# Pairwise bilinear products: from batch rows on the partitions to products computed transposed, with W stationary

## The chip, the core and the metric

The kernel runs on one NeuronCore of a Trainium2 chip. The core has five engines with queues of their own: TensorE (PE; its weight loads are PEld), VectorE (DVE), ScalarE (ACT), GpSimd (POOL) and SyncE (SP). Transfers between the device's memory (DRAM) and the on-chip memory (SBUF, 128 partitions) are issued from the queues of SP, ACT and POOL and carried by 16 DMA engines. TensorE writes its results to PSUM, which has eight banks of 512 float32 per partition. The metric is the device time of one execution in microseconds; work on the host isn't in it.

## The reference

The input is x, 4096 batch rows of 32 fields with 64 numbers each, and W, one 64 x 64 matrix for each of the 496 pairs of fields i < j. For each batch row and each pair, the vector of field i is multiplied with the pair's matrix, and the result elementwise with the vector of field j:

```python
i_idx, j_idx = np.triu_indices(32, k=1)
vi = inputs[:, i_idx, :]                      # (4096, 496, 64)
vj = inputs[:, j_idx, :]
vdotw = jnp.einsum('bpd,pde->bpe', vi, W)     # W: (496, 64, 64)
return (vdotw * vj).reshape(4096, -1)         # (4096, 31744)
```

All is float32. The output has 4096 x 31744 numbers, 520 MB; x has 33.6 MB and W 8.1 MB.

## The kernel before, in words

Batch rows lie on the partitions. The batch is cut into 32 tiles `t` of 128 rows. The output is kept as it is needed: for each row, the pairs in order, so that for a field i the columns of all j > i stand side by side.

**x.** `load_x` brings x in by 17 loads (`x_slots`, L35): one tile, fifteen times two tiles, and one. They land in `xbuf`, which has room for three tiles. A load of two tiles has 128 rows of 16,384 bytes. Most are issued on ACT's queue (L169). The six in `LIGHT_LOADS` go by POOL's queue through `load_beside` (L144) instead: two transfers that are cut so that the DMA engine numbered `LIGHT` carries none of it, since its eight rows are given in fours to two other engines. `PAIRS_FROM` says which two, in turn. Ahead of each of the two transfers, `from_engine` issues a small one ("nudge", L127) that moves POOL's round of engines to the one wanted. POOL's transfers are kept in program order.

**Transposes.** TensorE contracts over the partitions, so the 64 numbers of a field must lie on the partitions. `transpose_x` (L185) turns half a tile at a time: eight transposes of 128 x 128 on TensorE (L190) into two PSUM banks, and one copy by ScalarE to `xT` (L191). `xT` holds two fields per 128 columns, an even field on partitions 0 to 63 and the next on 64 to 127. The second half of a tile is turned at field pair `p` = 3, the first half of the next tile at `p` = 9 (L250 to L253).

**Products.** For a field pair `p` (fields 2p and 2p+1), the loop at L255 goes over the columns of W in pieces of up to 512. The stationary operand is 64 x 128 of `xT`, the moving one 64 x n of W, in SBUF as a whole (`w_sb`); the product lands as 128 batch rows x n columns (L262). The two fields use the two halves of TensorE's rows and two banks of the PSUM ring `pring`, so up to four steps are in flight. `multiply` (L195) lets DVE multiply both banks at once with the columns of x that stand beside (L203). Where the pieces of the two fields don't match, or where the ring wraps, it is done in parts (L203 again, or L211), which is why there are many shapes.

**Stores.** DVE writes into `ring`, 440 x 64 columns of SBUF. As soon as a third of it (147 or 146 units of 64 columns; in the first round four smaller parts) is written, `made` (L218) issues one store of 128 rows on SP's queue (L225). DVE may write into a third again when its store has landed.

**Start.** The first x tile and the next two go out on ACT's queue, W in five steps (six transfers) on SP's (L238, L240); the stores come behind W on SP's queue. A framework places the waits between engines from the order in which the program is written; each engine works in the order of the program.

On the host, x and W are only rearranged (L291 to L310).

Of the kernel before, what the change touches and what calls it, by code (L numbers as in the profile page):

```python
# [12 lines left out]
P = 128  # L13
# [3 lines left out]
ROUND = [147, 147, 146]  # L17
FIRST_ROUND = [118, 102, 110, 110]

LOADS = [[0], [1], [2, 3], [4, 5, 6], [7, 8, 9, 10, 11, 12, 13, 14, 15]]  # L20


FIRST_HALF_AT, SECOND_HALF_AT = 9, 3
RING_UNITS = sum(ROUND)
# [3 lines left out]
LIGHT_LOADS = [3, 5, 8, 10, 13, 15]  # L28
PAIRS_FROM = [5, 7, 9, 11, 13, 15, 1, 2, 0, 14, 12, 10, 8, 6]
HEAD = P // DMA_ENGINES  # L30
REST = HEAD // 2
PAD = 16


def x_slots(NT):  # L35


    loads = [[(0, 0)]]
    for t in range(1, NT, 2):
        if t + 1 == NT:  # L40
            loads.append([(t, 1)])
        elif loads[-1][-1] == (t - 1, 2):
            loads.append([(t + 1, 0), (t, 1)])
        else:
            loads.append([(t, 1), (t + 1, 2)])
    return loads
# [3 lines left out]
def pair_bilinear_kernel(  # L50
# [4 lines left out]
    out: bass.AP,  # L55
    F: int,
# [3 lines left out]

    nc = tc.nc
    NT = out.shape[1] * 2 // (F * (F - 1) * D)
    NPR = F // 2

    width = [(F - 1 - i) * D for i in range(F)]
    off = [sum(width[:i]) for i in range(F)]
    cols = sum(width)


    woff = [i % 2 * D + sum(width[i % 2 : i : 2]) for i in range(F)]
    ring_w = RING_UNITS * D
    ends = [0]
    while ends[-1] < NT * cols:
        for units in ROUND if ends[-1] else FIRST_ROUND:
            ends.append(min(ends[-1] + units * D, NT * cols))
            if ends[-1] == NT * cols:
                break
    missing = [b - a for a, b in zip(ends, ends[1:])]  # L100
    stored = 0
# [3 lines left out]

    ident = const.tile([P, P], F32, tag="ident", name="ident")
    make_identity(nc, ident)

    def runs(tl, a, b, n):

        ap = tl[:, a : a + n]
        return bass.AP(ap.tensor, ap.offset, [list(ap.ap[0]), [b - a, 2], list(ap.ap[1])])

    xbuf = const.tile([P, 3 * F * D], F32, tag="x", name="x")
    x_loads = x_slots(NT)
    pads = (DMA_ENGINES + 1) * PAD
    x_sizes = [
        P * len(load) * F * D + (pads if i in LIGHT_LOADS else 0) for i, load in enumerate(x_loads)
    ]
    slot = {t: xbuf[:, ts(s, F * D)] for load in x_loads for t, s in load}  # L120
# [8 lines left out]
    def from_engine(e):  # L129

        nonlocal cursor
        k = (e - cursor) % DMA_ENGINES
        if k:
            nudge = nudges[e == LIGHT + 1]
            if k == 1:
                from_pool(nudge[:3, :8], x[:64].rearrange("(g c) -> g c", g=2)[:, :12])
            else:
                from_pool(
                    nudge[:k].rearrange("p (h c) -> p h c", h=2)[:, :, :4],
                    x[: k * 8].rearrange("(p h c) -> p h c", p=k, h=2),  # L140
                )
        cursor = e

    def load_beside(at, xt, n_row, lap):  # L144

        nonlocal cursor
        most = DMA_ENGINES - 1
        for e, k, rows, p in (
            (PAIRS_FROM[lap % len(PAIRS_FROM)], 2, REST, most * HEAD),
            (LIGHT + 1, most, HEAD, 0),  # L150
        ):
            from_engine(e)
            n = rows * n_row
            blocks = x[at : at + k * (n + PAD)].rearrange("(k c) -> k c", k=k)
            from_pool(xt[p : p + k * rows], blocks[:, :n])
            at += k * (n + PAD)
            cursor = (e + k) % DMA_ENGINES

    def load_x(load):

        i = x_loads.index(load)
        at = sum(x_sizes[:i])
        n = len(load) * F * D
        s = load[0][1]
        xt = xbuf[:, s * F * D : s * F * D + n]
        if i in LIGHT_LOADS:
            load_beside(at, xt, n, LIGHT_LOADS.index(i))
        else:
            nc.scalar.dma_start(out=xt, in_=x[at : at + P * n].rearrange("(p c) -> p c", p=P))  # L169

# [3 lines left out]
    def take_banks(n):  # L174

        nonlocal bank
        if bank + n > BANKS:
            bank = 0
# [4 lines left out]
    xT = const.tile([P, NPR * P], F32, tag="xT", name="xT")  # L183

    def transpose_x(xt, g):  # L185

        n = 2 * BANK // P
        pt = take_banks(2)
        for c in range(n):
            nc.tensor.transpose(pt[:, ts(c, P)], xt[:, ts(n * g + c, P)], ident)  # L190
        nc.scalar.copy(xT[:, ts(g, 2 * BANK)], pt)  # L191

    ring = const.tile([P, ring_w], F32, tag="ring", name="ring")

    def multiply(tos, pm, xj, n):  # L195

        at = [to % ring_w for to in tos]
        cuts = {ring_w - a for a in at if a < ring_w < a + n}
        for i, j in zip([0, *sorted(cuts)], [*sorted(cuts), n]):
            a = [(to + i) % ring_w for to in tos]  # L200
            if len(tos) == 2 and a[0] < a[1]:
                xs = xj[:, i:j]
                nc.vector.tensor_tensor(  # L203
                    runs(ring, a[0], a[1], j - i),
                    runs(pm, i, BANK + i, j - i),
                    bass.AP(xs.tensor, xs.offset, [xs.ap[0], [0, 2], xs.ap[1]]),
                    ALU.mult,
                )
                continue
            for h, b in enumerate(a):  # L210
                nc.vector.tensor_tensor(  # L211
                    ring[:, b : b + j - i],
                    pm[:, h * BANK + i : h * BANK + j],
                    xj[:, i:j],
                    ALU.mult,
                )

    def made(a, b):  # L218

        nonlocal stored  # L220
        for i in range(stored, len(missing)):
            missing[i] -= max(0, min(b, ends[i + 1]) - max(a, ends[i]))
        while stored < len(missing) and not missing[stored]:
            a, b = ends[stored : stored + 2]
            nc.sync.dma_start(  # L225
                out=out[:, a:b], in_=ring[:, a % ring_w : a % ring_w + b - a]
            )
            stored += 1

    load_x(x_loads[0])  # L230
    w_sb = const.tile([P, sum(width[0::2])], F32, tag="w", name="w")
    done = 0
    for g in LOADS:

        upto = woff[2 * g[-1]] + width[2 * g[-1]]
        odd = woff[F - 1] + width[F - 1]
        both = min(upto, odd)
        nc.sync.dma_start(out=w_sb[:, done:both], in_=w[:, done:both])  # L238
        if both < upto:
            nc.sync.dma_start(out=w_sb[:D, both:upto], in_=w[:D, both:upto])  # L240
        done = upto

    transpose_x(slot[0], 0)
    for t in range(NT):
        xt = slot[t]
        for load in x_loads:
            if min(load)[0] == t + 1:
                load_x(load)
# [71 lines left out]
```

## Time and profile before

| | |
|---|---|
| time, median of 6 runs (lowest to highest) | 1319.6 us (1316.84 to 1319.89) |
| the profiled execution's own time | 1319.79 us |
| its span, first to last instruction | 1318.0 us |
| TensorE's granted clock | 0.962 |
| busy: PE, DVE, ACT, POOL | 1173.4, 1188.6, 66.1, 14.4 us |
| moved by DMA | 562.64 MB, 427 GB/s over the span |
| HBM read, written | 41.70 MB, 520.09 MB |
| matmul records on TensorE: products (L262), transposes (L190) | 4864, 512 |
| DVE instructions: L203, L211 | 1012, 471 |
| stores issued (L225) | 110 |

How to read it: the page gives each engine's busy time and its share of the span, then cuts the span into 40 equal slices (33 us here) with a digit for the busy tenths of each. "DMA" is the mean busy share of the 16 DMA engines, "GB/s" what they moved. The DMA queues are listed with packets, MB and their share of the time of 16 engines: q1 is SP's, q10 ACT's, q0 POOL's, q8 and q14 fetch instructions and tables. A chain is followed back from the last instruction, and its shares of the span are given by engine. A group of instructions is one line of the kernel, engine, operation and shape: number of instructions | busy time, mean ns of one | idle time of the engine before them, and what ended most of it. A float32 product shows as two records, each with a weight load. The mean of one is its latency, which is longer than the distance at which instructions follow each other. In a table of windows each row is a stretch of the span: its length, then the busy time of PE, PEld, DVE, ACT and POOL with the number of instructions, the granted clock, the DMA share and GB/s. A wait is given as engine, line <- what it waited for: total us, times, longest.

### The profile page before, as it was taken

The page shows a single profiled execution, that of the slowest core. Times are in us where ns is not written, and L with a number is a line of the kernel's source. Part 1 is how long each engine was busy: PE and PEld are TensorE (multiplying, and loading weights), DVE is VectorE, ACT ScalarE, POOL GpSimd, SP SyncE. Part 2 cuts the span into 40 slices and gives each one's busy share as a digit, 9 for nine tenths or more (in the row PEclk, how much of TensorE's full clock was granted, in tenths as well). Part 3 has the DMA queues.
Part 4 walks back from the last instruction along what each step waited for, and adds up shares of the span by engine and source line. Part 5 has one row for each costly group of instructions (what it writes and reads, how often), then busy time and mean ns, then how long its engine had stood idle before and what let it go on. Part 6 is the DMA issues. An engine that isn't in the chain of part 4 may idle for free.

```text
span 1318.0 us, 13125 instructions
## 1 busy us (share of the span) xinstructions
PE 1173.4 (89%) x5376; PEld 562.2 (43%) x5376; DVE 1188.6 (90%) x1483; ACT 66.1 (5%) x65; POOL 14.4 (1%) x30
## 2 busy tenths in 40 slices
PE   7999988989899998988989989898997989989992
PEld 3444335443444443444444444444444444434441
DVE  5999988989899998988989989898997999979993
ACT  1000000000000000000000000000000000000000
POOL 0000000000000000000000000000000000000000
PEclk9999998989899999998999989899998999989997
DMA  9999999999999999999999999999999999999998
GB/s 394 432 431 434 428 415 432 430 434 435 417 430 430 431 433 432 431 427 434 427 431 434 422 434 426 430 434 426 430 431 420 430 415 431 431 429 429 429 431 373
DMA packets 20012, 562.64 MB, mean 427 GB/s; under 512 B 2992, under 2 KB 2992, under 8 KB 3312
## 3 DMA queue, kind: packets, MB, share of 16 engines
q1 hardware_dynamic: 16640, 528.24, 93.4%
q10 hardware_dynamic: 1584, 20.97, 3.8%
q0 software_dynamic: 1728, 12.59, 2.4%
q8 instruction: 42, 0.69, 0.2%
q14 instruction: 18, 0.15, 0.0%
HBM read 41.70 MB, written 520.09 MB: 426 GB/s over the span
## 4 chain that ended last, share of the span: by engine, by line
DMA 44%; DVE 40%; issue 8%; PE 6%; POOL 0%; DVEq 0%; ACT 0%
DMA out_dram<-ring 36%; DVE ring L203 33%; DMA x<-in_x_dram 8%; DVE ring L211 7%; PE pring L262 5%; PE pring L190 1%; DVEq L203 0%; POOL x L127 0%; POOL nudge L127 0%; ACT xT L191 0%; DVEq L316 0%; DVEq L211 0%
## 5 line engine op out<-in xcount | busy, mean ns | idle before, releaser
L262 PE MATMUL pring<-w,xT 64*128 64x512 f32 (+4 forms) x4864 | 1108.9, 563 | 95.4 <-DVE ring L203 68.8
L203 DVE TENSOR_TENSOR ring<-pring,x 128x1024 f32<-128x1024 f32 (+4 forms) x1012 | 1043.5, 1092 | 79.5 <-DMA out_dram<-ring 44.4
L262 PEld LDWEIGHTS pring<-w,xT 64*128 64x128 f32 x4864 | 505.3, 191 | 656.8 <-DVE ring L203 441.7
L211 DVE TENSOR_TENSOR ring<-pring,x 128x64 f32<-128x64 f32 (+7 forms) x471 | 168.6, 412 | 28.6 <-DMA out_dram<-ring 20.4
L191 ACT COPY xT<-pring 128x1024 f32<-128x1024 f32 x64 | 64.8, 1012 | 1203.6 <-PE pring L190 1164.5
L190 PE MATMUL pring<-ident,x 128*128 128x128 f32 x512 | 72.6, 286 | 25.8 <-DMA x<-in_x_dram 17.3
L190 PEld LDWEIGHTS pring<-ident,x 128*128 128x128 f32 x512 | 56.9, 144 | 75.5 <-DVE ring L203 53.1
L127 POOL DMA_DIRECT2D x<-in_x_dram x12 | 7.0, 586 | 1125.2 <-DVE ring L211 1125.2
L127 POOL DMA_DIRECT2D nudge<-in_x_dram x12 | 6.8, 566 | 0.3 <-issue 0.3
L191 ACT ACT_TABLE_LOAD x1 | 1.3, 1283 | 1.7 <-PEq L312 1.7
masks.py:199 POOL TENSOR_SCALAR_AFFINE_SELECT ident<-ident 128x128 f32<-128x128 f32 x1 | 0.3, 287 | 0.1
masks.py:197 POOL MEMSET ident<- 128x128 f32 x1 | 0.2, 204 | 0.3 <-POOLq L312 0.3
L312 POOL MEMSET const-bfloat16-1.0<- 128x1 bf16 x1 | 0.1, 101 | 0.0
L312 POOL MEMSET const-uint8-127<- 128x1 uint8 x1 | 0.1, 101 | 0.0
L312 POOL MEMSET const-float32-0.0<- 128x1 f32 x1 | 0.1, 98 | 0.2 <-issue 0.2
L312 POOL MEMSET const-float32-1.0<- 128x1 f32 x1 | 0.1, 98 | 0.0
## 6 DMA issues: line engine op xcount, KB each, us to landing
out_dram<-ring SPq DMA_DIRECT2D x70, 4704.0 KB, 20.6
out_dram<-ring SPq DMA_DIRECT2D x35, 4672.0 KB, 21.0
x<-in_x_dram ACTq DMA_DIRECT2D x9, 2048.0 KB, 20.9
x<-in_x_dram POOLq DMA_DIRECT2D x6, 1920.0 KB, 31.5
out_dram<-ring SPq DMA_DIRECT2D x2, 3520.0 KB, 17.1
out_dram<-ring SPq DMA_DIRECT2D x1, 3776.0 KB, 17.3
out_dram<-ring SPq DMA_DIRECT2D x1, 3264.0 KB, 17.6
w<-in_w_dram SPq DMA_DIRECT2D x1, 2112.0 KB, 26.9
```

Source lines behind the costliest of these rows:

```text
L127: tc.keep_in_program_order(nc.gpsimd.dma_start(out=out, in_=in_))
L190: nc.tensor.transpose(pt[:, ts(c, P)], xt[:, ts(n * g + c, P)], ident)
L191: nc.scalar.copy(xT[:, ts(g, 2 * BANK)], pt)
L203: nc.vector.tensor_tensor(runs(ring, a[0], a[1], j - i), runs(pm, i, BANK + i, j - i), bass.AP(xs.tensor, xs.offset, [xs.ap[0], [0, 2], xs ...
L211: nc.vector.tensor_tensor(ring[:, b : b + j - i], pm[:, h * BANK + i : h * BANK + j], xj[:, i:j], ALU.mult,)
L262: nc.tensor.matmul(pm[:, h * BANK : h * BANK + n], xT[h * D : (h + 1) * D, ts(p, P)], w_sb[h * D : (h + 1) * D, a : a + n], start=True, st ...
L312: nc = bacc.Bacc("TRN2", target_bir_lowering=False, num_devices=1)
```

## The change

The products are computed transposed: the columns of one W matrix lie on the partitions of the result, and the batch rows along its columns.

- The host hands over x transposed: `xbuf` holds, for one chunk of 512 batch rows, 16 pieces (field pairs) of 512 columns, each with two fields on the two halves of the partitions. Which field is on which half alternates with the pair (`row_half`). There are eight chunks (`NC`) in place of 32 tiles. The same copy of x is TensorE's moving operand and DVE's multiplier; the transposes, the identity, ScalarE's copies and `xT` are gone.
- W is the stationary operand: for a step of two field pairs p < q, two products of 64 x 128 with 64 x 512 (field 2p and 2p+1, each with both fields of q), on the two halves of TensorE's rows. A step within pairs, (p, None), does two pairs of 64 x 64 in each of its two banks, and needs two DVE instructions on half the partitions each, where the other steps need one. `steps_of` gives 124 steps per chunk, in groups of four field pairs: the group with itself, then with each later group.
- x is loaded by 32 loads of 1 MB (a chunk's group of four pairs; 128 rows of 8,192 bytes). The four of chunk 0 go out first, on ACT's queue. A group of the next chunk is loaded over the old one when the last step that reads it has been issued. Nine loads go by POOL's queue as before (`LIGHT_LOADS`).
- The ring is three tiles of 20, 18 and 18 blocks of 512 columns, each stored as a whole by one transfer on SP's queue (in two halves in the first round). A tile is written again when its store has landed.
- W is loaded in five steps of 8, 16, 24, 32 and 44 blocks of 128 columns. The output leaves the chip in the order of the steps; the host puts it in order.

The diff, cut to its core:

```diff
-ROUND = [147, 147, 146]
-FIRST_ROUND = [118, 102, 110, 110]
-LOADS = [[0], [1], [2, 3], [4, 5, 6], [7, 8, 9, 10, 11, 12, 13, 14, 15]]
-FIRST_HALF_AT, SECOND_HALF_AT = 9, 3
-RING_UNITS = sum(ROUND)
+GROUP = 4
+W_STEPS = [8, 16, 24, 32, 44]
+SLOTS = [20, 18, 18]
 DMA_ENGINES = 16
 LIGHT = 4
-LIGHT_LOADS = [3, 5, 8, 10, 13, 15]
-PAIRS_FROM = [5, 7, 9, 11, 13, 15, 1, 2, 0, 14, 12, 10, 8, 6]
+LIGHT_LOADS = [(1, 0), (2, 0), (3, 0), (3, 2), (4, 0), (5, 0), (6, 0), (6, 2), (7, 0)]
+PAIRS_FROM = [5, 7, 9, 11, 13, 15, 1, 6, 8]
...
+def steps_of(NPR):
+    steps = []
+    for g in range(0, NPR, GROUP):
+        steps.append((g, None))
+        for h in range(g, NPR, GROUP):
+            for p in range(g, g + GROUP):
+                steps += [(p, q) for q in range(max(h, p + 1), h + GROUP)]
+    return steps
+
+def row_half(p, i):
+    return (i + p) % 2
+
+def x_loads(B, NPR):
+    return [(c, g) for c in range(B // BANK) for g in range(NPR // GROUP)]
...
+    xbuf = const.tile([P, NPR * BANK], F32, tag="x", name="x")
+    for g in range(NPR // GROUP):
+        load_x((0, g))
+    w_sb = const.tile([P, len(steps) * P], F32, tag="w", name="w")
+    done = 0
+    for n in W_STEPS:
+        cols = slice(done * P, (done + n) * P)
+        nc.sync.dma_start(out=w_sb[:, cols], in_=w[:, cols])
+        done += n
...
-        for c in range(n):
-            nc.tensor.transpose(pt[:, ts(c, P)], xt[:, ts(n * g + c, P)], ident)
-        nc.scalar.copy(xT[:, ts(g, 2 * BANK)], pt)
...
+    for c in range(NC):
+        for s, (p, q) in enumerate(steps):
+            pm = take_banks(2)
+            if made == base + room:
+                turn += 1
+                base, room = made, SLOTS[turn % len(SLOTS)]
+                tag = f"slot{turn % len(SLOTS)}"
+                osb = ring.tile([P, room * BANK], F32, tag=tag, name=tag)
+            a = (made - base) * BANK
+            for k in range(2):
+                if q is None:
+                    for h in range(2):
+                        pair = p + 2 * k + h
+                        m = row_half(pair, 2 * pair)
+                        o = row_half(pair, 2 * pair + 1)
+                        nc.tensor.matmul(
+                            pm[o * D : (o + 1) * D, ts(k, BANK)],
+                            w_sb[m * D : (m + 1) * D, s * P + k * D : s * P + (k + 1) * D],
+                            x_of(pair, m), start=True, stop=True)
+                else:
+                    m = row_half(p, 2 * p + k)
+                    nc.tensor.matmul(pm[:, ts(k, BANK)], w_sb[m * D : (m + 1) * D, ts(s, P)],
+                                     x_of(p, m), start=True, stop=True)
+            if q is None:
+                for h in range(2):
+                    rows = slice(h * D, (h + 1) * D)
+                    nc.vector.tensor_tensor(
+                        strided(osb[rows, a : a + BANK], BANK), strided(pm[rows, :BANK], BANK),
+                        strided(x_of(p + 1 - h, h), 2 * BANK), ALU.mult)
+            else:
+                nc.vector.tensor_tensor(
+                    strided(osb[:, a : a + BANK], BANK), strided(pm[:, :BANK], BANK),
+                    strided(x_of(q), 0), ALU.mult)
+            made += 2
+            half = turn < len(SLOTS) and made - base == (room // 2 + 1) // 2 * 2
+            if half or made in (base + room, blocks):
+                nc.sync.dma_start(out=out[:, stored * BANK : made * BANK],
+                                  in_=osb[:, (stored - base) * BANK : (made - base) * BANK])
+                stored = made
+            last = s + 1 == len(steps) or steps[s + 1][0] // GROUP != p // GROUP
+            if last and c + 1 < NC:
+                load_x((c + 1, p // GROUP))
```

`x_of(p, h)` is the piece of pair p in `xbuf` (all partitions, or half h), `strided(ap, step)` the same columns twice at a distance of `step`. `load_beside`, `from_engine` and `load_x` work as before, on the new loads.

## The prediction

> **What bounds the kernel now.** I read the page's slices first, then the DMA queues, then the chain that ended last.
>
> ```profile
> DMA  9999999999999999999999999999999999999998
> GB/s 394 432 431 434 428 415 432 430 434 435 417 430 430 431 433 432 431 427 434 427 431 434 422 434 426 430 434 426 430 431 420 430 415 431 431 429 429 429 431 373
> DMA packets 20012, 562.64 MB, mean 427 GB/s; under 512 B 2992, under 2 KB 2992, under 8 KB 3312
> q1 hardware_dynamic: 16640, 528.24, 93.4%
> q10 hardware_dynamic: 1584, 20.97, 3.8%
> q0 software_dynamic: 1728, 12.59, 2.4%
> q8 instruction: 42, 0.69, 0.2%
> DMA 44%; DVE 40%; issue 8%; PE 6%; POOL 0%; DVEq 0%; ACT 0%
> ```
>
> The row of nines says that the DMA engines are full from the first slice to the last but one, at 430 GB/s give or take a few. The output alone is 520 MB. The chain names VectorE (DVE) for 40%, so next: has DVE room?
>
> ```profile
> L203 DVE TENSOR_TENSOR ring<-pring,x 128x1024 f32<-128x1024 f32 x708 | 833.8, 1217 | 40.1 <-DMA out_dram<-ring 21.2 <-PE pring L262 8.2 <-DVE ring L203 1.2
> L262 PE MATMUL pring<-w,xT 64*128 64x512 f32 x3072 | 858.6, 635 | 75.0 <-DVE ring L203 57.1 <-DVE ring L211 12.3
> ...
> 1272.01 12.47 DVE L203 TENSOR_TENSOR ring<-pring,x 128x1024 f32<-128x1024 f32 x12
> ...
> DVE ring L203 <- DMA out_dram<-ring: 44.4, 19, 7.2
> ...
> PE pring L190 <- DMA x<-in_x_dram: 17.3, 4, 8.5
> ```
>
> The first two are groups by form, the third the timeline of DVE, the last the list of waits. Running freely, DVE makes a 128x1024 product in 12.47/12 = 1.04 us; it is busy 1188.6 us of 1318 and waits 44.4 + 20.4 us for stores (L203, L211). So DVE is ahead of the stores, but not by much. The windows show where the DMA engines lose (last columns: DMA share, GB/s):
>
> ```profile
> 40.00:88.00 48.00, 45.51 (x225) 21.72 (x222) 47.55 (x63) 3.04 (x3) 0.00 (x0) 1.00 1.01 434
> 173.00:200.00 27.00, 21.00 (x94) 8.05 (x92) 20.00 (x23) 1.01 (x1) 0.00 (x0) 0.94 1.02 415
> 254.00:270.00 16.00, 14.40 (x67) 6.60 (x66) 13.71 (x17) 1.01 (x1) 0.00 (x0) 1.00 1.00 432
> 337.00:363.00 26.00, 21.44 (x88) 10.22 (x88) 21.45 (x23) 1.01 (x1) 0.00 (x0) 0.87 1.01 421
> 1012.00:1032.00 20.00, 19.49 (x90) 10.72 (x91) 17.76 (x27) 0.98 (x1) 0.00 (x0) 0.90 0.97 417
> 1063.00:1081.00 18.00, 16.89 (x80) 6.86 (x78) 17.75 (x19) 1.01 (x1) 0.00 (x0) 1.00 1.01 421
> 1224.00:1238.00 14.00, 13.37 (x62) 5.73 (x58) 13.11 (x18) 1.01 (x1) 0.00 (x0) 1.00 1.00 422
> 1297.00:1318.00 21.00, 0.00 (x0) 0.00 (x0) 0.00 (x0) 0.00 (x0) 0.00 (x0) 0.56 0.79 339
> ```
>
> Stores alone run at 432 to 434 (1240:1297 has 432); I take 433. While x comes in through POOL's queue (173, 337) the rate falls to 415 and 421 with the share still at 1.0: packets take longer. Through ACT's queue the loss is small (254: none) to middling (1063, 1224). At 1012:1032 the share is 0.97: some engines have no store. The waits of that stretch say why: POOL's x landed after 32.9 us, the transposes (L190) waited 4.4 us for it, and DVE 5.4 us for TensorE.
>
> An account of the span: 562.64 MB / 433 GB/s = 1299.4 us. Head, 393 GB/s over the first 32 us: 40/433 x 32 = 3.0. Last 21 us, 339 GB/s: 4.6. The six POOL loads (windows from 173, 337, 577, 737, 980, 1143; 415, 421, 424, 422, 422, 426 GB/s over 25 to 28 us): 4.2. The nine ACT loads in mid-run (432, 432, 431, 433, 423, 420, 424, 421, 422 GB/s over 14 to 21 us): 2.2. The late stretch at 1012: 0.7. Sum 1314.1; 3.9 of 1318.0 stays unassigned, in small dips. The execution took 1319.79 us, 1.8 more than its span; the median of the six is 1319.6, so I add 1.6 to a span.
>
> **What the Trainium skill says.** "DMA: Bandwidth & Descriptors", section "Where 436 GB/s comes from", gives 435.2 GB/s as the ceiling of the 16 ports: the trace's 430 to 435 agrees, so the rate has no room. Its "Issuing engines are not separate DMA queues" says that SP's, ACT's and POOL's transfers share the same 16 engines; the trace agrees (share 1.0 with one queue or two). "Queues, rings and completion order" says that an engine alternates between queues packet by packet; I use this for how long a load lasts beside stores, and the trace's landings (20.9 us for 2048 KB by ACT) fit it.
>
> **The change part by part.**
>
> Bytes. Output and x are the same. W is 124 x 128 x 128 x 4 B = 8.13 MB; the six W loads add up to 7952 KB = 8.14 MB. The instruction queues bring 0.84 MB; q8's 0.69 MB is 10752 x 64 B, TensorE's 5376 + 5376 records. A product is two records before (2432 products, 4864 records). After there are 8 x (120 x 2 + 4 x 4) = 2048 products, so 8192 records: 0.16 MB less, with DVE's and ACT's some 0.2 MB, 0.46 us. Before, the lightened POOL loads spare one engine 6 x 8 x 16,384 B = 0.79 MB; after, 9 x 8 x 8,192 B = 0.59 MB: also 0.2 MB less. If that engine does the fetching, the gain is nil; I count -0.2 (0 to -0.46).
>
> x rows of 8,192 instead of 16,384 B. In the trace's packet records 16,384 B take 611 ns and 8,192 B 309: 7 ns more for two halves. Rows go from 2176 to 4096: 1920 x 7 / 16 engines = +0.8 us.
>
> x loads beside stores. In mid-run POOL goes from six of 2.1 MB to nine of 1.05, ACT from nine (eight of 2.1 MB, one of 1.05) to nineteen of 1.05. If the loss goes with bytes: POOL 4.2 x 0.75 = 3.2, ACT 2.2 x 19.9/17.8 = 2.5, together -0.7. If with the number of loads: POOL 4.2 x 9/6 = 6.3, ACT 2.2 x 19/9 = 4.6, together +4.5. For bytes: POOL loads lose over their whole 25 us and ACT's mostly nothing, so it is something each packet meets. For number: the only 1 MB load in mid-run, at 1224, lost 11/433 x 14 = 0.36 us, as much as a load of 2 MB. I take bytes, and keep +4.5 as the other end.
>
> DVE and TensorE. DVE: 8 x (120 + 4 x 2) = 1024 products of 1024 columns (the diagonal ones on half the partitions, at full price) x 1.04 = 1065 us against 1188.6 now; at the busy mean of 833.8/708 = 1.18 it would be 1206. TensorE: 3072 records of 64x512 were busy 858.6 us, so 1.12 for a pair of products (four records) with back-pressure; 992 pairs plus 32 more for the diagonals make 1145. Transposes (72.6) and ScalarE's copies (64.8) go. All stay below 1299, covered by the stores; without that cover DVE's gain would be up to 124. What it and the earlier x (below) buy is the late stretch: -0.7.
>
> Ring. 56 blocks of 2 KB per partition against 55 before, in 3 slots; a slot is free only when its store has landed. DVE needs 28 x 1.03 x 1.04 = 30 us for a round, the stores 56 x 0.262 MB / 433 = 34 plus loads. Two slots (some 23 us) lie queued. Nothing lost.
>
> Head. The first multiply no longer waits for transposes and copy (first transpose 8.48, first DVE 13.43 us). But stores stand behind W on SP's queue, and x and W are now 4.19 + 8.13 = 12.3 MB = 28.5 us of DMA from some 2 us on, against 11.3 MB. The first ten blocks need six DVE instructions, done by about 17 us: the store waits for the queue, not the reverse. Same bytes overall: 0 (-0.5 to +0.5). The four ACT and five SP issues are some 0.5 us each, hidden by the transfers.
>
> Reloads. A load waits on ACT's or POOL's queue for DVE's last use; nothing else is queued there but later loads. At 1318/992 = 1.33 us per step the shortest notice is group 8's: seven steps to the chunk's end and 23 of the next, 40 us (group 4: 37 steps, 49 us). Estimate of a landing: 8 rows per engine, each behind a store row of 40,960 B (1392 ns x 40,960/37,632 = 1.52): 8 x 1.83 = 15 us, 22 where two engines take 12 rows; POOL's loads of twice the bytes took 31.5 us (median) to 32.9. In time, so no stretch like 1012.
>
> Tail. The last store is 4 blocks, 8,192 B rows, as now: 0. Stores are 110 in both.
>
> Sum: -0.2 + 0.8 - 0.7 - 0.7 = -0.8: span 1317.2, time 1318.8.
>
> **Rivals.** (1) Faster: the loss beside loads comes from engines out of step after late stores, and goes as DVE gains room. For it: the dip at 1063 follows the late stretch at 1012. Against it: the load at 337 loses 0.7 us although DVE is ahead there and waits 3.8 us for a store. Two thirds of 6.4, and 1.0 of the unassigned: -0.2 + 0.8 - 0.7 - 4.3 - 1.0 = -5.4, 1314.2. (2) Slower: each load has a fixed price, so 28 in mid-run cost more than 15: -0.2 + 0.8 - 0.7 + 4.5 = +4.4, 1324.0. It decides (+2.6 us) from an extra 2.7 us, 0.21 for each of 13 further loads; 0.36 was seen for one. (3) A reload comes late and TensorE stops; the queued slots hide 20 us, beyond that each of 7 chunks pays. At 5 us each: 1354. The 40 us of notice speak against it. (4) One DMA engine ends late because the lightening no longer matches the fetches: 0.2 MB on one engine is 0.2/27 GB/s = 7 us; if half of it shows, 1323. The equal 0.2 MB above speak against it. That the change would leave the transposes or the extra copies in isn't possible by its code.
>
> **How the numbers follow.** No change can be told from about 0.2% (2.6 us; the six runs lie within 3.1). Mine: 0.50, with its own range 1316 to 1321.5; rival 1: 0.25; rival 2: 0.15; rival 3: 0.03; rival 4: 0.07. Mine is mostly "same" (0.42) with 0.06 faster and 0.02 slower. Rival 1 is faster (0.24), rivals 2 and 4 slower or just within (0.03). Faster 0.30, same 0.46, slower 0.24. The range, 1313.5 to 1324.5, holds nearly all of mine, two thirds of rival 1 and half of 2 and 4.
>
> **What would show it.** The row of nines unchanged; DVE busy near 1065 with long waits for stores (over 150 us); no window with a DMA share below 0.99 between head and tail; POOL-load windows of about 415 to 425 GB/s but shorter; no TensorE wait for x after the head. Wrong: a mid-run rate of stores alone other than 433, reload waits on TensorE, a last stretch in which few engines still move bytes, or 28 dips as deep as the old 15.

## The result, and the profile after

The changed kernel takes 1315.28 us (median of 16 runs, 1314.29 to 1316.73) against 1318.65 us for the kernel before (36 runs, 1316.47 to 1323.29; the six of the table above are among them): the ratio is 0.9975, 95% interval 0.9969 to 0.9982. That is 3.4 us less. The forecast was 1318.8 us with a range of 1313.5 to 1324.5; its likeliest case had 0.8 us of gain. The profiled execution took 1315.93 us with a span of 1313.8 us.

The page of the changed kernel, its slices, queues and chain:

```profile
DMA  9999999999999999999999999999999999999998
GB/s 392 430 437 429 433 430 434 431 432 430 436 428 434 430 428 428 431 431 428 435 425 440 423 436 426 437 430 427 435 424 434 428 431 431 424 434 434 432 433 354
DMA packets 22507, 562.41 MB, mean 428 GB/s; under 512 B 3648, under 2 KB 3648, under 8 KB 3776
q1 hardware_dynamic: 16560, 528.23, 93.6%
q10 hardware_dynamic: 3312, 24.12, 4.4%
q0 software_dynamic: 2592, 9.45, 1.8%
q8 instruction: 32, 0.52, 0.1%
DMA 65%; DVE 31%; issue 1%; PE 1%; DVEq 0%
```

The row of nines is unchanged: the DMA engines still bound the kernel. What differs is small. The lowest mid-run slice is 423 GB/s, where it was 415. The instruction fetches on q8 are 32 packets, where they were 42. The last slice is lower, 354 GB/s after 373. In the chain, DMA's share went from 44% to 65%, DVE's from 40% to 31%.

Groups by line, DVE's timeline near the end, and the list of waits:

```profile
L207 DVE TENSOR_TENSOR slot<-pring,x 128x1024 f32<-128x1024 f32 x960 | 1095.6, 1216 | 105.4 <-DMA out_dram<-slot 98.6
L200 DVE TENSOR_TENSOR slot<-pring,x 64x1024 f32<-64x1024 f32 x64 | 77.9, 1218 | 14.8 <-PE pring L181 11.5
...
1242.54 11.41 DVE L207 TENSOR_TENSOR slot<-pring,x 128x1024 f32<-128x1024 f32 x10 [1.79 <-DMA out_dram<-slot]
...
DVE slot L207 <- DMA out_dram<-slot: 98.6, 62, 5.2
PE pring L181 <- DMA x<-in_x_dram: 7.6, 1, 7.6
```

DVE makes ten products in 11.41 us, 1.14 us each, and is busy 1171.2 us in all, 17 us less than before and not 124 less. The diagonal products on 64 partitions (L200) cost the same 1.22 us of latency as those on 128. DVE waits 98.6 us for stores (L207) where it waited 44.4 + 20.4. TensorE waits for x once, in the head.

The windows of the changed kernel (length, busy PE, PEld, DVE, POOL, clock, DMA share, GB/s):

```profile
0.00:32.00 32.00, 24.41 (x84) 7.14 (x84) 20.66 (x19) 0.88 (x5) 1.00 0.96 391
159.00:186.00 27.00, 24.72 (x96) 7.45 (x96) 25.93 (x23) 0.00 (x0) 0.99 1.00 427
241.00:264.00 23.00, 19.19 (x68) 5.12 (x68) 19.86 (x19) 0.00 (x0) 1.00 1.01 432
319.00:347.00 28.00, 22.69 (x86) 7.25 (x84) 25.06 (x23) 0.00 (x0) 0.94 1.02 437
481.00:510.00 29.00, 23.64 (x84) 6.88 (x84) 25.11 (x23) 0.00 (x0) 0.90 1.00 420
967.00:994.00 27.00, 21.08 (x80) 5.76 (x76) 21.69 (x20) 0.00 (x0) 0.97 1.01 422
1046.00:1071.00 25.00, 21.55 (x78) 6.72 (x76) 22.82 (x21) 0.00 (x0) 0.93 0.99 423
1240.00:1290.00 50.00, 43.40 (x160) 12.74 (x156) 47.44 (x42) 0.00 (x0) 0.97 1.00 433
1297.00:1313.80 16.80, 0.00 (x0) 0.00 (x0) 0.00 (x0) 0.00 (x0) 0.50 0.64 275
```

A POOL load that runs alone costs nothing in one place (241, 432 GB/s) and some in another (1046, 423), and ACT's loads (159, 319) cost nothing to a little. The two deep dips left, 420 and 422, are where a POOL load and an ACT load run at the same time (loads (3, 2) with (3, 3), and (6, 2) with (6, 3)). The last 16.8 us move only 275 GB/s; the last 16.8 us of the kernel before moved 316.

An account that needs no reference rate comes from the packet records of the traces. Packets of 8,192 B and 37,632 B have a usual duration of 309 and 1392 ns, which gives 7.6 ns + 36.8 ps per byte; what a packet takes beyond this is its lengthening. A row of a transfer is one packet here. All is us, a mean over the 16 engines; fetches overlap with stores on their engine, and what is counted twice is taken off. The sum is the time of the last store packet.

| us | before | after | e6 | e8 | e2 | e7 | e11 |
|---|---|---|---|---|---|---|---|
| packets at their usual duration | 1301.4 | 1302.6 | 1301.4 | 1302.9 | 1301.3 | 1302.4 | 1301.3 |
| instruction and table fetches | 2.9 | 2.1 | 2.6 | 2.8 | 2.1 | 2.1 | 2.1 |
| lengthening in the first 32 us | 1.4 | 1.3 | 1.3 | 1.4 | 1.1 | 1.2 | 1.0 |
| lengthening of x rows after it | 2.5 | 0.2 | 1.8 | 1.8 | 0.9 | 0.1 | 0.9 |
| of store rows beside loads | 4.8 | 3.4 | 4.4 | 4.5 | 3.7 | 2.4 | 3.9 |
| of store rows elsewhere | 2.7 | 1.9 | 2.5 | 2.0 | 2.0 | 1.8 | 2.1 |
| counted twice | -4.4 | -5.0 | -4.4 | -4.9 | -4.6 | -4.9 | -4.6 |
| engines idle in the first 30 us | 2.0 | 2.0 | 2.1 | 2.0 | 2.2 | 2.2 | 2.2 |
| idle in between | 1.0 | 0.0 | 0.2 | 0.3 | 0.1 | 0.0 | 0.2 |
| idle in the last 25 us | 2.6 | 3.6 | 2.9 | 3.1 | 5.1 | 2.7 | 6.0 |
| end of the last store packet | 1316.7 | 1312.2 | 1314.7 | 1315.9 | 1314.1 | 1310.1 | 1315.2 |

(e2 to e11 are experiments below.) From before to after: x rows -2.3, stores beside loads -1.4, stores elsewhere -0.8, idle in between -1.0, fetches -0.8; against it more rows and semaphores +1.2 and a longer end +1.0 (the rest is mostly what is counted twice).

Each column is one execution, and executions differ: the profiled one of the kernel before took 1319.79 us, 1.1 more than the median, that of e11 1.9 more than its own, that of e8 1.7 less. Experiments that leave a kernel nearly as it was show how much one column can tell. By the same reckoning e9 (the kernel before with other store rows) has x rows lengthened by 2.0 us, store rows by 6.1 where the kernel before has 4.8 + 2.7, 0.3 us idle in between, 2.7 at the end, and its last store packet ends at 1314.2. Near copies of the changed kernel (e3, e5b, e10) have 0.2 to 0.3, 4.5 to 5.5, 0.0 and 4.1 to 4.2, and end at 1312.0 to 1313.1. So what repeats is that x rows are held up less, that fetches take less, and that the end is longer. More than a microsecond of the difference in store rows, and most of the idle time in between, is no larger than what the kernel before and its near copy differ by.

### The profile page after: what moved, and what is told of

It is laid out like the page before. It is cut to its first block, busy times and chain, and to the rows that moved or that the text cites. A ratio compares the mean times of both kernels' runs of the same rounds, so it can differ in the third digit from the quotient of the medians.

```text
span 1313.8 us, 9765 instructions
## 1 busy us (share of the span) xinstructions
PE 1137.7 (87%) x4096; PEld 335.0 (25%) x4096; DVE 1171.2 (89%) x1024; POOL 20.7 (2%) x40
## 2 busy tenths in 40 slices
DMA packets 22507, 562.41 MB, mean 428 GB/s; under 512 B 3648, under 2 KB 3648, under 8 KB 3776
## 4 chain that ended last, share of the span: by engine, by line
DMA 65%; DVE 31%; issue 1%; PE 1%; DVEq 0%
DMA out_dram<-slot 64%; DVE slot L207 29%; DVE slot L200 2%; DMA x<-in_x_dram 1%; PE pring L181 1%; PE pring L190 0%; DVEq L207 0%; DVEq L269 0%; DVEq L200 0%
## 5 line engine op out<-in xcount | busy, mean ns | idle before, releaser
L190 PE MATMUL pring<-x,w 64*128 64x512 f32 x3840 | 1074.3, 655 | 140.9 <-DVE slot L207 105.4
L207 DVE TENSOR_TENSOR slot<-pring,x 128x1024 f32<-128x1024 f32 x960 | 1095.6, 1216 | 105.4 <-DMA out_dram<-slot 98.6
L190 PEld LDWEIGHTS pring<-x,w 64*128 64x128 f32 x3840 | 319.1, 193 | 896.7 <-DVE slot L207 764.9
L200 DVE TENSOR_TENSOR slot<-pring,x 64x1024 f32<-64x1024 f32 x64 | 77.9, 1218 | 14.8 <-PE pring L181 11.5
L181 PE MATMUL pring<-x,w 64*64 64x512 f32 x256 | 66.1, 638 | 9.3 <-DMA x<-in_x_dram 7.6
L181 PEld LDWEIGHTS pring<-x,w 64*64 64x64 f32 x256 | 15.9, 139 | 55.5 <-DVE slot L207 26.8
L91 POOL DMA_DIRECT2D x<-in_x_dram x18 | 10.5, 585 | 1021.6 <-PE pring L190 1021.6
L91 POOL DMA_DIRECT2D nudge<-in_x_dram x18 | 10.1, 562 | 0.9 <-POOLq L265 0.9
## 6 DMA issues: line engine op xcount, KB each, us to landing
x<-in_x_dram ACTq DMA_DIRECT2D x23, 1024.0 KB, 18.6
x<-in_x_dram POOLq DMA_DIRECT2D x9, 960.0 KB, 28.2
```

The costliest lines, as they stand in the source:

```text
L91: tc.keep_in_program_order(nc.gpsimd.dma_start(out=out, in_=in_))
L181: nc.tensor.matmul(pm[o * D : (o + 1) * D, ts(k, BANK)], w_sb[m * D : (m + 1) * D, s * P + k * D : s * P + (k + 1) * D], x_of(pair, m), st ...
L190: nc.tensor.matmul(pm[:, ts(k, BANK)], w_sb[m * D : (m + 1) * D, ts(s, P)], x_of(p, m), start=True, stop=True,)
L200: nc.vector.tensor_tensor(strided(osb[rows, a : a + BANK], BANK), strided(pm[rows, :BANK], BANK), strided(x_of(p + 1 - h, h), 2 * BANK), A ...
L207: nc.vector.tensor_tensor(strided(osb[:, a : a + BANK], BANK), strided(pm[:, :BANK], BANK), strided(x_of(q), 0), ALU.mult,)
```

## The experiments

Three theories were set against each other (a fourth, C, between A and B, is stated with e8). A: the loads of x became smaller (1 MB, rows of 8,192 B), and that alone is the gain. B: the gain is what transposed products take away (transposes, late x, DVE's time). D, formed later: the gain is that store rows now begin at round addresses. Unless a kernel is named, "changed" means the changed kernel.

**Small loads in the kernel before.**

```diff
-    loads = [[(0, 0)]]
-    for t in range(1, NT, 2):
...
+    loads = [[(t, t % 3)] for t in range(NT)]
-LIGHT_LOADS = [3, 5, 8, 10, 13, 15]
-PAIRS_FROM = [5, 7, 9, 11, 13, 15, 1, 2, 0, 14, 12, 10, 8, 6]
+LIGHT_LOADS = [2, 5, 7, 10, 12, 15, 17, 20, 22, 25, 27, 30]
+PAIRS_FROM = [5, 7, 9, 11, 13, 15, 1, 6, 8, 10, 12, 14]
```

> The kernel before, but x in 32 loads of one tile (1 MB, rows of 8,192 B; twelve of them by POOL's queue) in place of 15 of two tiles; nothing else. Theory A: the loss beside loads comes from the size of the loads, and the changed kernel's gain is their halving; then this takes 1315 to 1316.5 us, the windows beside loads rise to 428 to 433 GB/s, the account's 6.4 us beside loads falls to under 4. Theory B: the gain comes from what the transposed products take away (transposes, late x, DVE's many shapes); then this stays at 1318 to 1319.5 us with dips as before.

It took 1322.06 us, ratio 1.0031 (1.0020 to 1.0041), outside what any theory expected. The windows of this kernel's head show why:

```profile
0.00:14.00 14.00, 3.28 (x12) 2.41 (x14) 0.00 (x0) 2.29 (x2) 3.64 (x11) 1.00 0.92 320
14.00:24.00 10.00, 8.29 (x30) 3.20 (x26) 8.26 (x8) 0.00 (x0) 0.00 (x0) 1.00 0.97 242
```

Tile 2's place in `xbuf` is free from the start, so its load, POOL's, went out at once and ran beside W: 242 GB/s with the engines busy, and the first slice fell from 394 to 326 GB/s. In the account, the lengthening in the first 32 us is 6.3 us in place of 1.4. So this run can't decide on A. It was repeated with the first POOL load later (e8):

```diff
-LIGHT_LOADS = [2, 5, 7, 10, 12, 15, 17, 20, 22, 25, 27, 30]
+LIGHT_LOADS = [4, 7, 9, 12, 14, 17, 19, 22, 24, 26, 28, 30]
```

> As the kernel before with 32 loads of one tile, but the first POOL load is that of tile 4, so that none runs beside W in the head (there the first slice had fallen from 394 to 326 GB/s, 5 us). The rest of that run lost less beside its loads than the kernel before. Theory C (load size is worth 1 to 2 us, less 0.8 for the extra rows; the rest of the gain is from the transposed products): 1316.5 to 1318 us. Theory A (it is the whole gain): 1315 to 1316 us. Theory B (load size is worth nothing): 1319 to 1320 us, for the extra rows.

1320.67 us, ratio 1.0013 (1.0002 to 1.0024): a little above even what B expected; small loads by themselves don't make the kernel before faster. A falls, and C (1316.5 to 1318) with it. Its 14 runs scatter widely, from 1317.56 to 1326.28 us, for a reason not looked for, and the profiled one is among the faster. In the table above the rows of x in this run are lengthened by 1.8 us, and 0.8 of it falls in one load, at 905 us, in a stretch in which stores run a little short (the engines' idle time in between is 0.3 us for the whole run):

```profile
0.00:32.00 32.00, 21.71 (x94) 10.50 (x96) 17.47 (x18) 3.31 (x3) 1.39 (x7) 1.00 0.96 392
870.00:930.00 60.00, 57.20 (x254) 28.39 (x253) 57.27 (x73) 3.77 (x4) 2.26 (x4) 0.95 1.00 420
```

**Big loads in the changed kernel.** (The change is in six places; its core:)

```diff
-    return [(c, g) for c in range(B // BANK) for g in range(NPR // GROUP)]
+    return [(c, g) for c in range(B // BANK) for g in range(0, NPR // GROUP, 2 if c else 1)]
-LIGHT_LOADS = [(1, 0), (2, 0), (3, 0), (3, 2), (4, 0), (5, 0), (6, 0), (6, 2), (7, 0)]
+LIGHT_LOADS = [(1, 0), (2, 0), (4, 0), (5, 0), (7, 0)]
...
-                load_x((c + 1, p // GROUP))
+                if p // GROUP % 2:
+                    load_x((c + 1, p // GROUP - 1))
```

> The changed kernel, but from the second chunk on x in loads of two groups (2 MB, rows of 16,384 B, five of them by POOL's queue); nothing else. Theory A: the loss comes back, 1317.5 to 1319 us, windows beside POOL loads at 415 to 426 GB/s. Theory B: 1315 to 1316 us as the changed kernel. A reload that comes too late would show as TensorE waiting for x in the later chunks.

1316.51 us, ratio 0.9982 (0.9973 to 0.9991), between the two; the interval overlaps the changed kernel's. The dips beside POOL loads are back, in the size that A expected:

```profile
127.00:155.00 28.00, 20.93 (x76) 5.42 (x72) 21.58 (x20) 0.00 (x0) 0.93 1.00 420
610.00:638.00 28.00, 23.40 (x84) 7.25 (x84) 22.59 (x20) 0.00 (x0) 0.94 1.00 420
```

but 1.3 us less for rows and semaphores make up for part of them, and most of the gain over the kernel before stays. TensorE waited for x in the head only. The edit also changes the balance of the engines: its five POOL loads keep 0.66 MB off the spared engine, where the changed kernel's nine keep 0.59 MB off it, and the engines are idle 5.1 us at the end in place of 3.6. What of its microsecond belongs to the size and what to the balance can't be told from it.

**Two POOL loads moved.**

```diff
-LIGHT_LOADS = [(1, 0), (2, 0), (3, 0), (3, 2), (4, 0), (5, 0), (6, 0), (6, 2), (7, 0)]
+LIGHT_LOADS = [(1, 0), (2, 0), (3, 0), (3, 1), (4, 0), (5, 0), (6, 0), (6, 1), (7, 0)]
```

> The changed kernel, but the two POOL loads (3, 2) and (6, 2), which run beside ACT's load of the next group, are (3, 1) and (6, 1), which run alone. Theory A (loss grows with the share of reads at one time): the dips of 420 and 422 GB/s at 481 and 967 us go, 1313.5 to 1314.5 us. Theory B: no difference, 1315.3 us.

1314.98 us, ratio 0.9977 (0.9967 to 0.9987): no difference from the changed kernel that this can tell. The dips themselves went, as this kernel's windows show:

```profile
481.00:510.00 29.00, 25.68 (x88) 7.67 (x88) 27.24 (x24) 0.00 (x0) 0.88 1.02 434
967.00:994.00 27.00, 21.62 (x82) 6.03 (x80) 22.70 (x20) 0.00 (x0) 0.96 1.01 432
```

In the account, store rows beside loads were lengthened by 2.8 us in place of 3.4, and the engines were idle 4.1 us at the end in place of 3.6. A reading that fits, but was not tested: what a dip gives back to some engines doesn't shorten the run if another engine is the last.

**The kernel before without transposes.** Those of later tiles are left out, so that W is multiplied with tile 0's rows for every tile; the output is another.

```diff
-            if p == SECOND_HALF_AT:
+            if p == SECOND_HALF_AT and not t:
-            if p == FIRST_HALF_AT and t + 1 < NT:
+            if p == FIRST_HALF_AT and t + 1 < 1:
```

> The kernel before with the transposes and copies of the first half tile alone and the second half of tile 0; the others are left out, so that later tiles are multiplied with tile 0's transposed rows, and the output is another. x is still loaded and multiplied with. Theory A: only the late stretch goes, 1317.5 to 1319 us. Theory B: most of the gain, 1315 to 1316 us.

1317.93 us, ratio 0.9998 (0.9989 to 1.0006), where B expected 1315 to 1316. The transposes and copies were worth at most 1.5 us, though TensorE did 41 us less. Windows of this kernel:

```profile
173.00:200.00 27.00, 20.61 (x88) 7.33 (x86) 21.18 (x25) 0.00 (x0) 0.00 (x0) 0.95 1.00 422
1012.00:1032.00 20.00, 19.28 (x86) 9.50 (x86) 19.36 (x25) 0.00 (x0) 0.00 (x0) 0.89 0.99 427
1063.00:1081.00 18.00, 13.87 (x58) 5.48 (x54) 14.21 (x16) 0.00 (x0) 0.00 (x0) 0.91 1.02 440
```

The stretch at 1012 no longer has late stores (427 GB/s for 417, and 440 for 421 at 1063). The dip beside the POOL load at 173 (422) stays. That the late stretch came with the transposes, as the prediction read it, isn't shown by this: e9 below keeps them, and its profile has no such stretch either.

**A burden on DVE.** Twice; the first was placed badly.

```diff
+            if s % 4 == 0:
+                nc.vector.tensor_tensor(spare, spare, spare, ALU.mult)
             made += 2
```

> The changed kernel with one more DVE product of 128x64 on a spare tile every fourth step (248 of them, some 0.13 us each, 32 us in all), left out of the output. DVE's busy time goes from 1171 to about 1203 us, above the 1188.6 us of the kernel before. If DVE's room is what the change gained by, 1318 to 1320 us; if not, 1315 to 1316 us.

1347.01 us, ratio 1.0211 (1.0198 to 1.0224). The added products depend on nothing but each other, and the framework put them early. DVE's timeline of this kernel, and two windows:

```profile
60.26 0.74 DVE L216 TENSOR_TENSOR spare<-spare 128x64 f32<-128x64 f32 x3
60.92 1.22 DVE L209 TENSOR_TENSOR slot<-pring,x 128x1024 f32<-128x1024 f32 x1
62.05 0.47 DVE L216 TENSOR_TENSOR spare<-spare 128x64 f32<-128x64 f32 x2
...
60.00:90.00 30.00, 19.98 (x72) 5.43 (x72) 28.97 (x67) 0.00 (x0) 1.00 0.60 259
300.00:400.00 100.00, 88.78 (x326) 26.39 (x325) 92.25 (x82) 0.00 (x0) 0.97 1.00 430
```

Two or three of them stand behind every product from 60 to 160 us. All 248 start before 153 us. DVE then needs some 1.7 us for two blocks where the stores need 1.2, so it falls behind the stores, and the DMA share falls to 0.60. Elsewhere nothing is lost (430 GB/s). It shows what DVE costs where it does bound, and not what its room is worth. So it was tied to the step:

```diff
+            if s % 8 == 1:
+                nc.vector.tensor_tensor(spare, pm[:, :64], x_of(p)[:, :64], ALU.mult)
             made += 2
```

> The changed kernel with a further DVE product of 128x64 after every eighth step (128 of them, some 0.2 us each, 26 us), on the step's own bank and a spare tile, so that it stays in its place; left out of the output. DVE's busy time then is 1195 to 1200 us, a little over the 1188.6 of the kernel before. If DVE's 17 us less are what the change gained by: 1318 to 1320 us. If not: 1315 to 1316 us, with DVE's waits for stores down from 101 to about 75 us.

1316.37 us, ratio 0.9981 (0.9974 to 0.9989). The page's first part and a wait:

```profile
PE 1139.8 (87%) x4096; PEld 328.6 (25%) x4096; DVE 1186.9 (90%) x1152; POOL 20.7 (2%) x40
...
DVE slot L208 <- DMA out_dram<-slot: 86.3, 54, 4.8
```

DVE is as busy as in the kernel before (1186.9 and 1188.6 us) and the time is still 2.2 us below it. DVE's total isn't the cause of more than a small part of the gain: the interval overlaps the changed kernel's.

**Round addresses.** Both ways:

```diff
-ROUND = [147, 147, 146]
-FIRST_ROUND = [118, 102, 110, 110]
+ROUND = [144, 144, 144]
+FIRST_ROUND = [112, 96, 112, 112]
```

> The kernel before with a ring of 432 units in thirds of 144 (first round 112, 96, 112, 112): every store row is then 36,864 B and begins at a multiple of 4,096 B of the output row (the first round's at multiples of 4,096 too), as in the changed kernel, in place of 37,632 and 37,376 B at multiples of 256. Nothing else. Theory D (a store whose rows begin off the round addresses is slower beside loads, and the changed kernel gains by its round ones): 1315 to 1317 us, and packets beside loads as short as in the changed kernel. Otherwise: 1319 to 1320 us, as before or a little more for the smaller ring.

```diff
-                    out=out[:, stored * BANK : made * BANK],
+                    out=out[:, LEAD + stored * BANK : LEAD + made * BANK],
...
-    o_d = nc.dram_tensor("out_0_dram", (P, blocks * BANK), F32, kind="ExternalOutput").ap()
+    o_d = nc.dram_tensor("out_0_dram", (P, blocks * BANK + SPARE), F32, kind="ExternalOutput").ap()
```

> The changed kernel, but the output rows on the device are 4,096 B longer and the results begin 256 B into them, so that no store row begins at a multiple of 4,096 B. Theory D: the loss beside loads comes back, 1317 to 1319 us. Otherwise: 1315.3 us.

The kernel before with round rows, and a ring of 432 units in place of 440: 1318.2 us, 0.9995 (0.9987 to 1.0003). The changed kernel with shifted ones: 1315.95 us, 0.9982 (0.9975 to 0.9988), with x rows lengthened by 0.2 us as in the changed kernel. D falls.

The first of the two also shows something of the late stretch. Its transposes are all there, and once they waited for x longer than those of the kernel before did at 1012. Its longest such wait after the head, and the windows at 1012 and 1063:

```profile
PE pring L190 <- DMA x<-in_x_dram: 5.1, 1, 5.1
...
1012.00:1032.00 20.00, 18.90 (x92) 9.33 (x90) 19.87 (x29) 1.01 (x1) 0.00 (x0) 1.00 0.99 426
1063.00:1081.00 18.00, 14.33 (x56) 6.21 (x56) 13.50 (x15) 1.01 (x1) 0.00 (x0) 0.81 1.02 435
```

(The wait falls between 1140 and 1180 us.) Yet its DMA engines were idle only 0.3 us between head and end, where they were idle 1.0 in the kernel before. So a late x of 4 to 5 us doesn't always hold up the stores, and the late stretch may belong to one execution of the kernel before more than to the kernel.

**Three undone at once.** e2, e5b and e10 each stood a little above the changed kernel's ratio, with intervals that overlap its own. All three edits together:

> The changed kernel with three earlier edits at once: x from the second chunk on in loads of two groups (2 MB), the output 256 B into longer rows, and a further DVE product of 128x64 (left out of the output) after every eighth step. Each alone gave back 0.6 to 0.7 thousandths of the changed kernel's 2.5. If the gain is a sum of such small terms, they add: ratio 0.9993 to 0.9998, 1317.7 to 1318.3 us. If each was the scatter of its own runs: ratio 0.9975 to 0.9985, 1315.3 to 1316.6 us.

1316.34 us, ratio 0.9982 (0.9975 to 0.9989). They don't add. What they give back together is no more than each did alone (and may be the balance that e2 changes, which is changed here too), and seven tenths of the gain stay with big loads, a busy DVE and odd addresses.

**The lightened engine.** Without POOL loads, and with seven:

```diff
-LIGHT_LOADS = [(1, 0), (2, 0), (3, 0), (3, 2), (4, 0), (5, 0), (6, 0), (6, 2), (7, 0)]
+LIGHT_LOADS = []
```

> The changed kernel with all x loads on ACT's queue, no POOL load and no nudge, so that all DMA engines carry the same x bytes. If one engine does the fetches of instructions (32 packets of 16,384 B and some of 8,192: 20 to 24 us of that engine), it ends each store late, the ring waits for it and the time is 1326 to 1336 us. If the fetches are spread, the time is 1312 to 1315 us, since the POOL loads' losses are gone.

1327.63 us, ratio 1.0065 (1.0051 to 1.0080), so 12 us above the changed kernel. With equal bytes of x and output on all engines, one engine ends the stores late. A store brings 16 semaphores, one from each engine. In the store issued at 875 us the last comes 10.6 us after the mean of the 16, while the others lie between -1.4 and +1.0 us (in the changed kernel's store at 868 us the 16 lie between -3.0 and +2.3). The lag builds up, 5.1 us in a store at 312 us and 7.5 at 521, and has a median of 8.3 us over the 110 stores, where it is 2.6 in the changed kernel. Every slot of the ring waits for the last one; in the account the engines are idle 4.7 us between head and end and 8.9 at the end (0.0 and 3.6). The records don't name the engine. Windows of this kernel, in mid-run and at the end:

```profile
700.00:740.00 40.00, 35.89 (x134) 9.79 (x130) 37.11 (x33) 0.00 (x0) 1.00 0.99 419
1220.00:1260.00 40.00, 36.42 (x126) 11.52 (x128) 37.31 (x34) 0.00 (x0) 0.91 0.96 415
1314.00:1320.00 6.00, 0.00 (x0) 0.00 (x0) 0.00 (x0) 0.00 (x0) 0.50 0.45 191
```

The share is 0.96 to 0.99 in mid-run, as the other engines run out of stores, and falls to 0.45 near the end.

```diff
-LIGHT_LOADS = [(1, 0), (2, 0), (3, 0), (3, 2), (4, 0), (5, 0), (6, 0), (6, 2), (7, 0)]
+LIGHT_LOADS = [(1, 0), (2, 0), (3, 0), (4, 0), (5, 0), (6, 0), (7, 0)]
```

> The changed kernel with seven POOL loads, the two that run beside an ACT load, (3, 2) and (6, 2), being ACT's now. The two dips of 420 and 422 GB/s go (-1.5 us of rate), but the engine that is spared carries 2 x 65,536 B more, 4.8 us. If that engine is the fetching one and was just balanced, 1317 to 1320 us; if it had room, 1313.5 to 1314.5 us.

1313.34 us, ratio 0.9957 (0.9945 to 0.9969): faster than both kernels (its five runs, 1313.08 to 1313.88, all lie below the 16 of the changed kernel). Windows of this kernel:

```profile
481.00:510.00 29.00, 23.53 (x88) 6.67 (x88) 26.91 (x24) 0.00 (x0) 0.99 1.02 436
967.00:994.00 27.00, 21.43 (x80) 6.18 (x78) 22.69 (x21) 0.00 (x0) 0.94 1.01 431
1294.00:1311.50 17.50, 0.00 (x0) 0.00 (x0) 0.00 (x0) 0.00 (x0) 0.50 0.74 317
```

The dips are gone (436 and 431 for 420 and 422), and the end is shorter (317 GB/s over 17.5 us for 275 over 16.8). In the table, stores beside loads take 1.0 us less and the end 0.9. Moving the two loads (e3) took the dips away too, without this gain. What e7 has beyond it, by the code: four engines that took 4 rows more in two loads each now do so in one (4 x 8,192 B are 1.2 us of an engine), and the spared engine carries 16 rows more. That this is the cause was not tested apart; e3 and e7 together suggest that nine light loads spare that engine more than it needs.

## Why the prediction was right or wrong

**As a whole.** 1315.28 us lies in the range, but below the 1316 to 1321.5 of its likeliest case; the range reached it because it took in rival 1. The base was high by 1.0 us (1319.6 from six runs, 1318.65 from 36), and of the 3.4 us gained it had forecast 0.8.

**The bound: right.** The DMA engines stayed full, and nothing on TensorE or DVE came to bound in the changed kernel. TensorE's 1145 us came close (1137.7).

**Bytes: right, and worth more than it said.** 562.64 MB became 562.41, q8 42 packets 32, as worked out. I valued it at 0.2 us, because I took the spared bytes to shrink with the need. The fetches take 0.8 us less in the account, and e4 with e7 show that one engine lags by 8 to 10 us without lightening and that seven light loads are enough. The 0.2 was too small by half a microsecond or so.

**Rows: right.** +0.8 us expected; the packets' usual duration without semaphores went from 1299.7 to 1300.5. Semaphores added 0.4, which I had left out.

**x loads beside stores: wrong in size and in the way it was argued.** I let 6.4 us scale with bytes (-0.7) or with number (+4.5). By the same windows it fell to 2.8, from 481:510 (13/433 x 29 = 0.9), 967:994 (0.7), 1046:1071 (423 GB/s, 0.6), 159:186 (0.4) and 803:831 (430, 0.2): -3.6. Neither scaling is borne out: e8 has the kernel before with small loads and no gain, e2 the changed kernel with big ones and a loss of about 1 us, if any. By these windows the term is most of what the forecast of 0.8 us lacked of 3.4. But windows of one execution differ by some GB/s from another's: the load at 1046 has 423 GB/s here and 431 in e3, which leaves it as it was. The records of x rows are the firmer sign, with 2.0 to 2.5 us in the kernel before and e9, and 0.2 to 0.3 in the changed kernel and its near copies.

**DVE: wrong by 106 us, without harm.** 1065 us expected, 1171.2 measured. The 12.47 us for twelve "128x1024" came from a line of the timeline that merges shapes and shows the first. Ten equal ones take 11.41. Among the twelve were one of 896 columns, one of 640 and one of 384. The busy mean of 1.18 beside it was the better number. DVE's room, which I thought to grow by 124 us, grew by 17; e5b shows that these were not what counted. The waits for stores, forecast at over 150 us, were 98.6 + 2.5.

**The late stretch: open.** -0.7 expected. In the changed kernel and its near copies no store is late in mid-run (idle in between 0.0, for 1.0 before). But e6 without the transposes has 0.2 and e9 with them 0.3, so most of the 0.7 may belong to the one execution that I read it from, and that the transposes make it is not shown.

**Head and reloads: right.** 391 GB/s in the first 32 us for 393, first store issued at 18.4 us behind W; POOL's loads landed in 28.2 us (median) where 40 were to spare. The landings themselves were estimated too short: 15 us for 18.6 by ACT's queue, 22 for 28.2 by POOL's.

**Tail: wrong by 1 us.** I said 0. Idle at the end went from 2.6 to 3.6 us (4.1 to 4.2 in the near copies). The engines are further out of step at the end: the 16 semaphores of the last store lie between -2.1 and +2.5 us of their mean before, and between -3.1 and +3.6 after.

**The rivals.** Rival 1 had the size: 1314.2 against 1315.28. Its mechanism isn't borne out. DVE's room grew by 17 us and wasn't the means (e5b), and where the kernel before has no late stretch (e6, e9) its x rows are still lengthened by 1.8 and 2.0 us. That it named the size was luck as far as the runs tell. Rival 2 didn't happen. Rival 3 neither. Rival 4's mechanism exists in part, as e4 shows: one engine does lag, and the slowest engine sets the pace. That it lags by its fetches is inferred. In the changed kernel the lightening covered it, by e7 with something to spare.

**What stays open.** Why x rows and stores are held up less in the changed kernel. Taken alone, none of the transposes, the size of the loads, DVE's time and the addresses accounts for it, and three of them undone together leave 1.8 of the 2.5 thousandths. Two things in the kernel before lengthen x rows in the records: POOL loads of 2 MB (e6 still has 1.8 us, 1.4 of it in them) and stretches short of stores (0.8 us in one load of e8). Each experiment took away one of the two; both at once was not tried. By the records of x rows the size of the loads and the transposed products each have a share: 2.0 to 2.5 us with big loads in the kernel before and e9, 0.9 after the head of e1 and 1.8 in e8 with small ones, 0.9 with big loads in the changed kernel (e2, e11), and 0.2 to 0.3 with small ones. The times don't show it as clearly. Nor was the kernel before with fewer light loads. This is a rival for the whole gain: the change also moved the balance of the engines (0.79 MB kept off the spared engine before, 0.59 after, with fewer fetches), and in e7 a shift of 0.13 MB, with the two dips gone as well, comes with 2 us.

## What to carry to other kernels

Where the DMA engines are full, less work on the other engines buys little by itself (here 41 us less of TensorE at most 1.5 us): look for what holds single packets up, and for which of the 16 engines ends last. When loads or instruction counts change, try the balance of the engines again; two light loads fewer came with 2 us here, more than half of the whole change. Where a change is worth a few microseconds, compare a profile with that of a near copy before reading a term of it. Don't take a duration from a line that may merge shapes.

## What the runs showed of the hardware that was not expected

- One DMA engine comes to lag when nothing is spared it, by 8.3 us in the median over the stores and 10.6 at most, in a kernel with 32 fetch packets of 16,384 B and 12 of 8,192 (e4); that this is the engine of the fetches was inferred, not seen.
- A POOL load beside W's loads, with no store in flight, brought the engines to 242 GB/s (e1); a POOL load alone beside stores cost nothing to 2% in the changed kernel (432 and 423 GB/s, where stores alone have 433).
- A POOL and an ACT load of 1 MB at the same time beside stores lower the rate to 420 and 422 GB/s (424 and 419 in e10), where one at a time leaves 423 to 437.
- DVE products of 1024 columns with one operand in PSUM, on 128 partitions, follow each other every 1.13 us (median of the changed kernel). Half the partitions make it no shorter: the second of two products on 64 partitions starts 1.22 us after the first, and the next on 128 partitions 1.26 us after that.
